# Two cross attentions in sequence: output products moved beside the last subtiles, folding of queries moved between stage 2's products

## The chip, the cores and the metric

The kernel runs on one core of one Trainium2 chip. The metric is the time of one execution in microseconds, measured on the device. All times below are microseconds unless marked ns. Engines are named as in the profile: PE (TensorE), DVE (VectorE), ACT (ScalarE), POOL (GpSimd), SP (SyncE, which here only issues DMAs).

## The reference

Two cross-attention layers follow each other on the same 4 x 64 context rows. All is float32; B = 4, 1024 query rows per batch, hidden size 1024.

```python
# layer 0: 32 query heads of 32, 8 key/value heads, biases, residual, layer norm
q = hidden @ Wq + bq; k = ctx @ Wk + bk; v = ctx @ Wv + bv
attn = softmax(q k^T / sqrt(32) + mask)          # 64 keys
x = (attn v) @ Wo + bo + hidden
x = (x - mean(x)) * rsqrt(var(x) + 1e-6) * gamma + beta
# layer 1: 16 heads of 64, context layer-normed, gated residual
a = layer_norm(ctx)
Q = x @ Wq1.T; K = a @ Wk1.T; V = a @ Wv1.T
attn = softmax(where(mask, Q K^T / 8, -inf))
y = x + tanh(gate) * (attn V) @ Wo1.T
```

## The kernel before

The 4096 rows are 32 subtiles of 128 (`t`), 16 pairs of two subtiles (`pair`), and 4 blocks of 8 subtiles, one batch each. The large products (1024 x 1024 by rows) are done in Winograd's form of Strassen's scheme: each 2 x 2 block product takes seven products instead of eight, with sums of blocks made ahead on DVE. `right_sums` makes the four sums of a weight, `left_out` the four of a left operand (128 x 512 each), and `products` lists the seven steps of one pair. A step is four 128-row matmuls over `HK`, each of which the profile records twice (so eight records), and then one DVE addition of the PSUM bank into the result rows `r` (L455). Three of the seven results are partial: the bank X takes four products on top of each other and is added to another quarter of the rows after each, V takes two, W one. A product that goes on in a bank must wait until DVE has read it.

The program runs in these parts.

- Setup: keys and values of both layers from the context.
- Stage 1: layer 0's queries for four blocks (`query_steps`, 28 steps a block). Beside the steps of blocks 1 to 3 run the attentions of subtiles 0 to 23.
- The last subtiles, 24 to 31: no query steps are left, so `other_work` gives them other steps.
- Stage 2: per pair the output projection of layer 0 (`project`, seven products with `w_o`), residual, bias and layer norm (`close_rows`), written to DRAM as `x1`.
- Stage 3: per pair layer 1's scores, softmax, and output. Layer 1's queries and keys are folded into one 1024 x 256 weight per batch (`ad`), its values and output weight into another (`bd`): `folded_queries` makes `ad`, `folded_values` makes `bd`.

`folded_queries(kT, wT, k)` handles one of eight chunks of 128 rows in four steps. A step has four matmuls on 64 partitions (two row halves side by side), 256 columns each, into two PSUM banks, two ACT copies out (L903), and, after every second step, a DMA of 1 MB to `ad` on POOL's queue (L909). `folded_values(vT, wch, c)` has two steps a chunk; each has two groups of two 64-partition matmuls with 512 columns (L924), four ACT copies (L929), and two DMAs on SP's queue.

`mix(t, count)` (L771) writes out one subtile of layer 0's attention and draws `count` steps of `other_work` at five places. A subtile's chain is: 16 score matmuls in two halves (`front`, L680, each followed by a DVE add with the mask, L684), the row maxima of both halves (`largest`, L691) and their subtraction (L694), exp on ACT, the row sums (`total`, L711), reciprocals and the division (`divide`, L715), the transposes of the previous subtile's probabilities on PE with copies by ACT (`flip`, L407 and L410), and the product with the values (L759) with two copies of ACT (L398) and a DMA. For some heads ACT does the subtraction itself, one head at a time, with the maximum as its bias, and sums up on the way (`some`, L698): the pair `alone` tells how many of the 16 heads of each half. In the last eight subtiles it is `(4, 0)`; the other heads go through DVE and one exp per half (`others`, L706).

`other_work` draws, after the query steps, 32 folding steps, eight of them before subtile 24 (`FOLD_AHEAD`), and then four products of pair 0 (`FIRST`). The loads of `w_o` (four blocks of 1 MB, four DMAs each, L147) are on SP's queue. After subtile 31 come pair 0's other three products, and then stage 2's loop from pair 1. In that loop `project` takes a list `fill` of small steps and runs a share of them after each product; the folding of values of chunk `pair - 1` (pairs 1 to 8) is part of that list.

PSUM has eight banks: `ps_big`, two tiles of two banks (scores, folding of values), and `ps_wx`, four tiles of one bank (products, folding of queries, transposes and values of the last subtiles). The weight pool has seven slots of 1 MB for tag `wa` (first `wq0`, then `wo0`) and seven for tag `wb`.

Instructions aren't issued in the order of the source: a scheduler orders them, engine by engine, by priorities and its own estimate of times, except where `keep_in_program_order` binds one.

Of the kernel before, what the change touches and what calls it, by code (L numbers as in the profile page):

```python
# [14 lines left out]
P = 128  # L15
# [4 lines left out]
B = 4  # L20
# [51 lines left out]
def tile_two_cross_attentions(  # L72
# [35 lines left out]
    ps_wx = ctx.enter_context(tc.tile_pool(name="ps_wx", bufs=4, space=bass.MemoryType.PSUM))  # L108
    ps_big = ctx.enter_context(tc.tile_pool(name="ps_big", bufs=2, space=bass.MemoryType.PSUM))

# [6 lines left out]
    def wx():  # L117
        return ps_wx.tile([P, 512], F32, tag="wx", name="wx")

# [21 lines left out]
    def block_of(w, i, j, tag, name, turned=False):  # L141
        t = new_block(tag, name)
        cols = slice(j * HW, (j + 1) * HW)
        if turned == "heads":
            rows = w.rearrange("(c g i e d) o -> c i e d g o", c=2, g=4, i=2, e=2)
            for a in range(NQ):
                nc.sync.dma_start(  # L147
                    out=t[a * Q : (a + 1) * Q], in_=rows[a // 2, a % 2, i][:, :, cols]
                )
# [285 lines left out]
    def products(a, w, r, bias=None, tail=None):  # L435
# [6 lines left out]
        def product(name, s, m, first, last):  # L442
            if first:
                banks[name] = wx()
# [33 lines left out]
        ]  # L478
        return [lambda o=o: step(*o) for o in order]

    def project(a, w, r, fill, bias=None, tail=None):

        share = -(-len(fill) // 7)
        for step in products(a, w, r, bias, tail):
            step()
            for _ in range(min(share, len(fill))):
                fill.pop(0)()
# [166 lines left out]
    def attend0(t):  # L654
# [13 lines left out]
        alone = BY_HEAD if by_turning(t) else (4, 0) if t >= NSUB - SUB else (0, 0)  # L668
# [218 lines left out]
    def folded_queries(kT, wT, k):  # L887
# [3 lines left out]
        def heads(cc):  # L891
            banks = [wx(), wx()]
# [47 lines left out]
    def load_o(pair, pool, tag="o2"):  # L940
        o = pool.tile([P, KC, 2 * P], F32, tag=tag, name=f"o2_{pair}")
        load = nc.sync.dma_start(out=o, in_=oTd[pair])
        if pair < 2:
            tc.keep_in_program_order(load)
        return o

    def load_outputs(pair):
        o = load_o(pair, o2pool) if pair > 1 else second if pair else load_o(0, early)
        r = []
        for u in range(2):  # L950
            t = pair * 2 + u
            ru = (rpool.tile([P, H], F32, tag="r", name=f"r_{t}") if pair
                  else early.tile([P, H], F32, tag="r", name=f"r_{t}", bufs=2))
            load = nc.sync.dma_start(out=ru, in_=x[sub_ap(t), :])
            if not pair:
                tc.keep_in_program_order(load)
            if pair:
                nc.gpsimd.tensor_tensor(ru, ru, bo_sb, ALU.add)  # L958
            r.append(ru)
        return o, r  # L960

    def other_work(rows):

        nonlocal fold, early, bo_sb, w_o, first, first_rows, second
# [12 lines left out]
        queries_cm.close()  # L977
        fold = open_pool(fold_cm, "fold", 1)

        early = open_pool(early_cm, "early", 1)  # L980
        kT = fold.tile([P, KC, B * S], F32, tag="kvT", name="kT")
        nc.sync.dma_start(out=kT, in_=kTd)
        wT = turned_chunk(0)
        w_o, w_o_loads = right_loads(wo0, "wa", "wo0", "heads")
        bo_sb = constant(bo0.partition_broadcast(P), [P, H], "bo", F32, fold)
        for k in range(KC):
            ahead = turned_chunk(k + 1) if k + 1 < KC else None
            for step in folded_queries(kT, wT, k):
                step()
                yield  # L990
            wT = ahead
            if k in (1, 2, 3, 4):
                w_o_loads[k - 1]()
            if k == 5:
                run(right_sums(w_o))
                o, first_rows = load_outputs(0)
                a = left_out(o, early, "0_0")
        second = load_o(1, wpool, "wb")

        def tail():  # L1000
            nonlocal ahead_a
            ahead_a = left_out(second, early, "0_1")


        first = products(a, w_o, first_rows, None, tail)
        for _ in range(FIRST):
            first.pop(0)()
            yield

    fold_cm, early_cm = ExitStack(), ExitStack()  # L1010
    fold = early = bo_sb = w_o = first = first_rows = second = ahead_a = ahead_r = None
    FIRST = 4
# [3 lines left out]
    AHEAD, FOLD_AHEAD = 4, 8  # L1016
# [11 lines left out]
    n = 4 * KC - FOLD_AHEAD + FIRST  # L1028
# [268 lines left out]
```

## Time and profile before

| what | us |
|---|---|
| median of three runs | 1914.9 (1913.46 to 1915.07) |
| the profiled execution | 1915.1 |
| its span, first to last instruction | 1913.3 |
| mean granted clock of PE | 0.995 of full |
| PE idle in the whole span | 44.4 |
| stage 1 with setup, to the first folding step | 0 to 588.9 |
| last subtiles, to subtile 31's last matmul of values | 588.9 to 716.4 |
| stage 2, to the last product of pair 15 | 716.4 to about 1185 |
| longest waits of PE: values for the transposed probabilities (DVE) | 6.2 in 5 |
| folding of queries for ACT's copies of transposes | 4.6 in 5 |
| folding of values for its own copies | 3.7 in 7 |

The profile is of one execution on the chip. A row of a group gives the source line, the engine, the operation, output and input tiles, shapes, the number of instructions, busy time and mean ns of one, the idle time ahead of them and who ended it. A row of the order in time gives start, duration, engine, line, operation and count; in brackets idle time before it and its releaser. PE's durations are modelled from pipelined records, so PE can look busy while it runs below its rate; the distance from one start to the next is the better measure.

### The profile page before, as it was taken

How to read it: one execution, taken by the hardware profiler on the slowest of the kernel's cores; microseconds unless marked ns; L12 is line 12 of the kernel's file. 1: busy time of each engine (PE TensorE's matmuls, PEld its weight loads, DVE VectorE, ACT ScalarE, POOL GpSimd, SP SyncE). 2: the span in 40 equal slices, each digit the busy share in tenths (PEclk: the TensorE clock that was granted, in tenths of full speed). 3: DMA queues.
4: the chain of work that ended last, by engine and by line, in shares of the span. 5: the costliest groups of instructions: out<-in, count | busy, mean ns of one | idle time of the engine just before them, and what ended most of it. 6: DMA issues, size and time to landing. Idle time of an engine off the chain costs nothing.

```text
span 1913.3 us, 17522 instructions
## 1 busy us (share of the span) xinstructions
PE 1868.9 (98%) x6096; PEld 880.0 (46%) x6096; DVE 1292.1 (68%) x1582; ACT 427.9 (22%) x1396; POOL 179.1 (9%) x212
## 2 busy tenths in 40 slices
PE   8999999999998899999999999999999999999999
PEld 7744444444455653343344444444444444444444
DVE  3425589789878985575568778557665766576653
ACT  1101575666536751212100001000000000000000
POOL 0016011111100103121113100000000000000000
PEclk9999999999999899999999999999999999999999
DMA  8996599899878966567473363466656565657421
GB/s 276 184 222 192 158 253 247 253 252 261 252 186 275 302 234 207 188 207 238 164 218 138 121 141 90 110 165 158 150 143 165 150 158 143 165 142 165 121 88 44
DMA packets 220745, 350.54 MB, mean 183 GB/s; under 512 B 26992, under 2 KB 146160, under 8 KB 215664
## 3 DMA queue, kind: packets, MB, share of 16 engines
q1 hardware_dynamic: 152896, 242.44, 45.8%
q0 software_dynamic: 15216, 60.83, 10.5%
q10 hardware_dynamic: 52544, 46.14, 8.8%
q8 instruction: 48, 0.79, 0.2%
q14 instruction: 41, 0.34, 0.1%
HBM read 207.53 MB, written 141.82 MB: 183 GB/s over the span
## 4 chain that ended last, share of the span: by engine, by line
PE 82%; DVE 8%; DMA 5%; issue 2%; ACT 2%; POOL 0%; SPq 0%; DVEq 0%; POOLq 0%; ACTq 0%
PE wx L446 59%; PE wx L576 14%; PE big L680 2%; DMA pq<-p 2%; PE big L924 1%; PE wx L379 1%; PE big L379 1%; DVE s L684 1%; PE big L759 1%; DMA p<-s 1%; DMA q<-qTd 1%; DVE s L715 1%; DVE mx L691 1%; DVE sm L711 1%; DMA o<-oTd 1%
## 5 line engine op out<-in xcount | busy, mean ns | idle before, releaser
L455 DVE TENSOR_TENSOR r<-wx,r 128x512 f32<-128x512 f32 x224 | 153.5, 686 | 230.1 <-PE wx L446 215.3
L698 ACT ACTIVATE s<-s,mx 128x64 f32<-128x64 f32 x488 | 162.8, 335 | 74.9 <-DVE mx L691 70.7
L502 ACT ACTIVATE s<-s 128x1024 f32<-128x1024 f32 x32 | 33.7, 1057 | 651.7 <-DVE s L501 651.7
L459 DVE TENSOR_TENSOR s<-wx,key_bias 128x512 f32<-128x512 f32 x64 | 44.1, 690 | 136.7 <-PE wx L446 136.7
L446 PE MATMUL wx<-wo_B,S 128*128 128x512 f32 x256 | 117.1, 600 | 1.5 <-DVE r L455 1.5
L576 PE MATMUL wx<-xT,wq_S 128*128 128x512 f32 x256 | 116.5, 598 | 0.8 <-ACT z L587 0.8
L446 PE MATMUL wx<-b_B,pT 128*128 128x512 f32 x256 | 115.8, 593 | 0.6 <-ACT pT L414 0.6
L446 PE MATMUL wx<-b_B,S_p 128*128 128x512 f32 x256 | 116.0, 596 | 0.0
L446 PE MATMUL wx<-a_B,xT 128*128 128x512 f32 x256 | 115.4, 592 | 0.0
L446 PE MATMUL wx<-a_B,S_x 128*128 128x512 f32 x256 | 115.3, 593 | 0.1
L576 PE MATMUL wx<-xB,wq_A 128*128 128x512 f32 x256 | 115.1, 597 | 0.0
L446 PE MATMUL wx<-wo_B,o 128*128 128x512 f32 x256 | 114.8, 596 | 0.0
L958 POOL TENSOR_TENSOR r<-r,bo 128x1024 f32<-128x1024 f32 x30 | 78.5, 2625 | 313.8 <-DMA r<-in_x_dram 159.4
L684 DVE TENSOR_TENSOR s<-big,m 128x1024 f32<-128x1024 f32 x64 | 77.4, 1215 | 28.4 <-PE big L680 26.8
L680 PEld LDWEIGHTS big<-kv,q 64*128 64x128 f32 x1024 | 71.1, 195 | 48.3 <-issue 39.9
L698 ACT ACTIVATION_READ_ACCUMULATOR s<-s,mx 128x1 f32 x488 | 91.4, 187 | 0.0
L680 PE MATMUL big<-kv,q 64*128 64x128 f32 x1024 | 82.6, 292 | 2.6 <-DMA q<-qTd 2.6
L419 DVE STREAM_TRANSPOSE pT<-pq 128x1024 f32<-128x1024 f32 x66 | 78.0, 1219 | 3.3 <-DMA pq<-p 3.3
L446 PEld LDWEIGHTS wx<-wo_B,S 128*128 128x128 f32 x256 | 47.1, 190 | 67.7 <-issue 51.2
L715 DVE TENSOR_TENSOR s<-s,sm 128x1024 f32<-128x1024 f32 x64 | 77.0, 1216 | 0.9
L446 PEld LDWEIGHTS wx<-wo_B,o 128*128 128x128 f32 x256 | 47.8, 190 | 63.5 <-issue 62.3
L446 PEld LDWEIGHTS wx<-a_B,S_x 128*128 128x128 f32 x256 | 48.5, 190 | 62.0 <-issue 58.4
(162 smaller groups left out, 2903.5 us busy)
## 6 DMA issues: line engine op xcount, KB each, us to landing
p<-s POOLq DMA_DIRECT2D x19, 1024.0 KB, 8.1
pq<-p POOLq DMA_DIRECT2D x76, 256.0 KB, 6.0
xq<-in_x_dram SPq DMA_DIRECT2D x64, 256.0 KB, 10.2
q<-qTd SPq DMA_DIRECT2D x32, 512.0 KB, 7.4
oTd<-oT ACTq DMA_DIRECT2D x32, 512.0 KB, 7.4
ad<-a POOLq DMA_DIRECT2D x16, 1024.0 KB, 8.9
o<-oTd SPq DMA_DIRECT2D x16, 1024.0 KB, 5.1
r<-in_x_dram SPq DMA_DIRECT2D x32, 512.0 KB, 5.3
```

The costliest lines, as they stand in the source:

```text
L379: nc.tensor.matmul(ps[:, 0:256], w[k // HK, c // HK][:, k % HK, sub_ap(c % HK)], ct[:, k, :], start=(k == 0), stop=(k == KC - 1),)
L419: return nc.vector.transpose(dst.rearrange("p k (u i) -> p k u i", i=Q), t[:, :, k0 * Q : k1 * Q].rearrange("p u (k j) -> p k u j", j=Q),)
L446: nc.tensor.matmul(banks[name], a[s][:, k, :], w[m][:, k, :], start=first and k == 0, stop=last and k == HK - 1, skip_group_check=True,)
L455: nc.vector.tensor_tensor(at, bank, at, ALU.add)
L459: nc.vector.tensor_tensor(at, bank.rearrange("p (h s) -> p h s", s=S), bias.unsqueeze(1).to_broadcast([P, 512 // S, S]), ALU.add,)
L502: nc.scalar.activation(s, s, AF.Exp)
L576: nc.tensor.matmul(bank, w_q[a][:, k, sub_ap(i)], rows[b][:, k, :], start=first and k == 0, stop=last and k == HK - 1, skip_group_check=True,)
L680: nc.tensor.matmul(ps[:, at : at + P], q[on, c * 4 + g, :], k0bd[on, b, c, :], start=True, stop=True,)
L684: nc.vector.tensor_tensor(quarters[:, :, c * 8 : (c + 1) * 8], ps.rearrange("p (k a l) -> p a k l", a=NQ, l=Q), mask.rearrange("p e (h l) ...
L698: nc.scalar.activation(heads[:, e, k], heads[:, e, k], AF.Exp, bias=mx[:, e, k : k + 1], accum_out=sm[:, e, k : k + 1],)
L715: nc.vector.tensor_tensor(heads[:, e], heads[:, e], wide(sm[:, e]), ALU.mult)
L958: nc.gpsimd.tensor_tensor(ru, ru, bo_sb, ALU.add)
```

## The change

- Between stage 1 and the last subtiles PSUM's four `wx` banks are shared out anew (`share_banks`): three for `wx` and one, `sum_bank`, for the products; from stage 2 on, four for `wx` again.
- The last subtiles take 12 of 32 folding steps (`FOLDED` = 3 chunks, four steps of them before subtile 24 instead of eight), and then products of pairs 0 and 1: seven and four (`BESIDE` = 2, `LEFT` = 3 left over). Their order puts X's four products in a row, then V's two, then W, so that one bank is open at a time (`one_bank`). The last three products of pair 1 stand around subtile 31's transposes and values.
- Stage 2's loop starts at pair 2. Folding of queries for chunks 3 to 7 goes there, in pairs 3 to 7: one step after each of four products, in the `big` banks. Folding of values goes to pairs 3 to 10, one step after each of two products (`beside`), and no longer through `fill`.
- `alone` is `(8, 4)` for the last subtiles: 12 of 32 heads are taken one at a time by ACT.
- The loads of `w_o` go to POOL's queue. The residual rows of pairs 0 and 1 are one DMA of 1 MB each into a `wb` slot, as are the left operands of pairs 0 to 2. `vT` has a tile of its own; the pools of stage 3 that took the place of `early` open at pair 11 instead of 3, and the first load of `ad` moves from pair 10 to 11.

```diff
+    def share_banks(name, sums):
+        nonlocal ps_wx, ps_sum
+        ps_cm.close()
+        ps_wx = ps_cm.enter_context(
+            tc.tile_pool(name=f"ps_wx{name}", bufs=4 - sums, space=bass.MemoryType.PSUM, reuse_waits="tile")
+        )
+        ps_sum = sums and ps_cm.enter_context(
+            tc.tile_pool(name=f"ps_sum{name}", bufs=sums, space=bass.MemoryType.PSUM, reuse_waits="tile")
+        )
+    def sum_bank():
+        return ps_sum.tile([P, 512], F32, tag="sum", name="sum") if ps_sum else wx()
...
-                nc.sync.dma_start(
+                nc.gpsimd.dma_start(
                     out=t[a * Q : (a + 1) * Q], in_=rows[a // 2, a % 2, i][:, :, cols]
...
-                banks[name] = wx()
+                banks[name] = sum_bank()
...
+        if one_bank:
+            order = [order[i] for i in (0, 1, 3, 4, 2, 5, 6)]
...
-        for step in products(a, w, r, bias, tail):
+        for i, step in enumerate(products(a, w, r, bias, tail)):
             step()
+            if i in beside:
+                beside[i]()
...
-        alone = BY_HEAD if by_turning(t) else (4, 0) if t >= NSUB - SUB else (0, 0)
+        alone = BY_HEAD if by_turning(t) else (8, 4) if t >= NSUB - SUB else (0, 0)
...
-            banks = [wx(), wx()]
+            banks = two() if pairs else [wx(), wx()]
...
+        share_banks("1", 1)
...
-        for k in range(KC):
+        for k in range(FOLDED):
-            for step in folded_queries(kT, wT, k):
+            for n, step in enumerate(folded_queries(kT, wT, k)):
                 step()
+                if k > 0 and n % 2 and sums:
+                    sums.pop(0)()
                 yield
...
+        for step in products(a, w_o, first[0][1], None, tail, True):
+            step()
             yield
+        for step in products(ahead_a[0], w_o, first[1][1], None, tail1, True):
+            steps.append(step)
+        while len(steps) > LEFT:
+            steps.pop(0)()
+            yield
+        rest.extend(steps)
...
-    AHEAD, FOLD_AHEAD = 4, 8
+    AHEAD, FOLD_AHEAD = 4, 4
...
+    counts = [4, 4] + [(i + 1) * (7 * BESIDE - LEFT) // 6 - i * (7 * BESIDE - LEFT) // 6 for i in range(6)]
     for i in range(SUB):
-        mix(last + i, (i + 1) * n // SUB - i * n // SUB)
+        mix(last + i, counts[i])
...
+    fill = close_with_bias(0, first[0][1]) + close_with_bias(1, first[1][1])
+    FROM = BESIDE + 1
-    for pair in range(1, NPAIR):
+    for pair in range(BESIDE, NPAIR):
...
+        beside = {}
+        k = pair - FROM + FOLDED
+        if pair >= FROM and k < KC:
+            ahead_w = turned_chunk(k + 1) if k + 1 < KC else None
+            beside.update(zip((0, 2, 3, 5), folded_queries(kT, wT, k, True)))
+            wT = ahead_w
+        k = pair - FROM
+        if 0 <= k < KC:
+            ahead_w = chunk(wo1, k + 1, "wo1") if k + 1 < KC else None
+            beside.update(zip((1, 4), folded_values(vT, wch, k)))
+            wch = ahead_w
...
-        project(a, w_o, r, fill, tail=tail)
+        project(a, w_o, r, fill, tail=tail, beside=beside)
```

## The prediction

> **What bounds the kernel now.** I read the engines' shares first, then the stretches around the change, then the order in time on VectorE and TensorE, then the waits.
>
> ```profile
> PE 1868.9 (98%) x6096; PEld 880.0 (46%) x6096; DVE 1292.1 (68%) x1582; ACT 427.9 (22%) x1396; POOL 179.1 (9%) x212
> ...
> 617.60:629.50 11.90, 10.87 (x100) 8.35 (x99) 11.34 (x12) 10.63 (x26) 1.51 (x2) 1.00 0.94 314
> 669.60:681.50 11.90, 10.78 (x99) 8.26 (x98) 11.31 (x13) 10.58 (x26) 1.50 (x2) 1.00 1.00 313
> 775.20:804.60 29.40, 28.87 (x73) 11.68 (x72) 16.38 (x25) 5.25 (x10) 5.66 (x2) 1.00 0.66 211
> ```
>
> The columns of a stretch are its length and then busy time of PE, weight loads, DVE, ACT, POOL. PE looks full everywhere, but in the last eight subtiles (590 to 716 us) that is stretched work: in 11.9 us DVE is busy 11.3. In stage 2 (the third stretch, one pair) DVE has 13 us to spare and PE none. So PE work that moves from stage 2 into the last subtiles is free as long as DVE, or the loop through ACT, isn't lengthened.
>
> One subtile on DVE, from row maximum to row maximum:
>
> ```profile
> 669.63 2.35 DVE L691 TENSOR_REDUCE mx<-s 128x16 f32<-128x1024 f32 x2
> 671.90 2.08 DVE L694 TENSOR_TENSOR s<-s,mx 128x768 f32<-128x768 f32 x2
> 674.53 2.17 DVE L711 TENSOR_REDUCE sm<-s 128x12 f32<-128x768 f32 x2 [0.55 <-ACT s L706]
> 676.62 0.37 DVE L712 RECIPROCAL sm<-sm 128x16 f32<-128x16 f32 x2
> 676.90 2.35 DVE L715 TENSOR_TENSOR s<-s,sm 128x1024 f32<-128x1024 f32 x2
> 679.17 2.35 DVE L684 TENSOR_TENSOR s<-big,m 128x1024 f32<-128x1024 f32 x2
> 681.55 2.35 DVE L691 TENSOR_REDUCE mx<-s 128x16 f32<-128x1024 f32 x2
> ```
>
> It takes 11.92: 11.1 of work and 0.85 of waits, 0.55 of them for ACT. The first maxima of subtiles 24 to 31 start at 602.3, 617.6, 629.5, 641.5, 658.1, 669.6, 681.6, 694.1: seven periods, 91.7 together, with a late load of q in the first and the sums of pair 0's left operand in the fourth. ACT has, in the same region:
>
> ```profile
> L903 ACT ACTIVATE a<-wx 128x512 f32<-128x512 f32 x64 | 33.7, 610 | 18.3 <-PE wx L897 13.9 <-DMA ad<-a 4.3
> L410 ACT COPY pT<-wx 128x512 f32<-128x512 f32 x32 | 16.9, 584 | 6.7 <-PE wx L407 6.7
> L698 ACT ACTIVATE s<-s,mx 128x64 f32<-128x64 f32 x32 | 10.8, 340 | 12.2 <-DVE mx L691 12.0
> L706 ACT ACTIVATE s<-s 128x768 f32<-128x768 f32 x8 | 6.8, 853 | 0.0
> ```
>
> And stage 2's joints, PE in order of time, with the wait that its folding of values has:
>
> ```profile
> 734.95 1.12 PE L924 MATMUL big<-wo,vT 64*128 64x512 f32 x2
> 736.01 3.70 PE L446 MATMUL wx<-wo_B,S 128*128 128x512 f32 x8
> 739.64 1.98 PE L924 MATMUL big<-wo,vT 64*128 64x512 f32 x6
> 741.55 3.70 PE L446 MATMUL wx<-wo_N,o 128*128 128x512 f32 x8
> ...
> 777.71 2.28 PE L924 MATMUL big<-wo,vT 64*128 64x512 f32 x8 [0.51 <-ACT b L929]
> ...
> PE big L924 <- ACT b L929: 3.7, 7, 0.6
> ```
>
> A product is eight matmul records. Seven of them take 24.67 in a pair without joints, 3.525 each; between two groups of 64-row matmuls one takes 3.63 (736.01 to 739.64), so a joint costs 0.1. Eight records of values take 1.92 standing alone, 2.97 when cut into 2 and 6 (1.06 + 1.91), and two groups in a row 4.74 with their wait, against 3.84.
>
> **The change, part by part.**
>
> *The last subtiles, in DVE's time.* Four heads fewer in both halves: a subtraction or sum takes 1.218 on 16 heads and 0.948 on 12, so 0.27 per four heads, four times a subtile: work falls from 11.1 to 10.0. Added: eleven sums of products instead of three before subtile 31's division (8 x 0.61 spacing), left operands of three pairs instead of one (8 more operations of 0.61, since the changed order brings pair 2's in too), and two bias adds (1.2 each) and three small statistics steps that the order pulls in: 4.9 + 4.9 + 3.9. Eight subtiles save 8.6 and take 13.7.
>
> *The loop through ACT.* ACT takes twelve single heads instead of four, at a spacing of 0.335 (timeline of ACT, 642.70 to 644.05 for four). From the end of a subtile's first maximum: four exps 1.34, three copies of transposes 1.42 (three follow in 1.42 at 684.15), the exp on 12 heads 0.78, the fourth copy 0.5, which now comes after it, because only three banks are left for four transposes; half of the values' matmuls 0.5, the rest of the next scores 0.3, hand-overs 0.25: the next first score add can start at 5.1, where DVE has been idle for some 0.5. From there one add 1.14, division 1.14, the sum on eight heads 0.6 (ACT is ready at 7.3), reciprocal 0.15, product sum 0.6, division, add and maximum 3.4: 12.15 a period. Walking the changed order through with those prices, the periods are 12.4, 15.9, 12.4, 14.2, 13.8, 13.9, 12.6, together 95.2. The second has ACT still folding (four steps, 4 x 1.0), pair 0's left operand and the first product's sum; the fourth five left-operand steps; the fifth and sixth the bias adds and statistics. DVE's own work and waits without the loop give about the same, 7 x 12.0 + 11.5 = 95.5. So +3.5.
>
> *The start* gains little: four folding steps fewer stand ahead of subtile 24 (PE is through at 593.8, not 597.7), but q was issued at 592.1 and landed no sooner than 5.6 later, and DVE had the weight sums until 597.6. I take -0.8, bounds 0 and -1.1 (DVE's idle time there).
>
> *The tail*, end of subtile 31's first maximum to its last values matmul: 21.1 before (695.3 to 716.4), full of five products. Now 16.9: division at 709, transposes 1.9, three quarters of a product 2.6, values 1.0. So -4.2; the stretch ends 1.5 earlier, and holds 13 products instead of six and 13 folding steps instead of 32.
>
> The sqrt of pair 0 gets between the exps of subtiles 30 and 31: two table loads of 1.28 (the row has one, after the last subtile), 3.3 with the sqrt and a DMA issue, in a gap of 4.2 before the next exp: hidden. The Trainium skill, "ScalarE: Activation LUTs", What ACT_TABLE_LOAD costs, adds a drain of about 1.4 to each: as an estimate two switches are then 5.3, 6.0 with the rest, the exps start 1.8 late, and the sum below would be -3.3; no row here shows the drain.
>
> *Stage 2.* Seven products leave: -24.7. Nineteen folding steps come: alone they took 0.96 to 1.00 (600.85 to 601.84), with a joint half the values' 1.92 would be 0.96, cut in two as the values are 1.49. I take 1.03, since all but one stand whole: +19.5, up to +28. Some 33 more joints at 0.106: +3.5, bounds 0 and 5. Values: chunks 1 to 4 lose their wait (4.74 to 3.84), chunks 5 to 7 are cut twice each in the changed order (4.74 to 5.94), the first loses a little: -0.9. The 0.97 that PE waited for POOL's bias add (L958) goes, as one folding piece more stands before it: -1.0, bound 0. Sum -3.6. DVE and ACT in this stage have 13 and 24 us of 29 free per pair; the 10 writes of `ad` (1 MB each) fall where the DMA share is 0.4 to 0.66. Each chunk is loaded a pair ahead. All value tiles share one slot; a write to `bd` has 6 to 8 us of slack before its slot is needed.
>
> *Queues.* The sixteen loads of wo0 go from SP to POOL. Four POOL loads issue in 2.18; POOL has nothing between 525 and 593, so 8.7 fit. One stands ahead of subtile 18's reads of `pq`; SP issued it at 523.4, the reads came at 525.4, so nothing, or 2 if the slot is late. SP loses a wait of 5.6 (four loads from 534.7) with `qTd` writes behind it: 0 to -2. Zero for both. On SP five loads of 1 MB now stand ahead of subtile 28's q; they have two periods, 24 us, for 13 us of DMA at 390 GB/s.
>
> **Sum.** -1.5 - 3.6 = -5.1: span 1908.2, and with the 1.8 around it (1915.1 measured, span 1913.3) 1910.0. The median of the runs shown is 0.2 below that execution, which is less than I can resolve.
>
> **Rivals.**
>
> *The loop decides and the kernel gets slower.* For: TensorE, DVE, ACT and PE's one sum bank now wait on each other in a ring, with 12 exps, three banks and two products per subtile; before, transposes' copies already held folding up 4.6 us in 5 waits, 0.92 each. If every subtile has one such wait and the spacings are the full durations (periods 13.7, 17.1, 13.2, 14.6, 13.8, 14.1, 12.9, which end the stretch 2.9 late), it is +2.9 + 7.4 - 3.6 = +6.7: 1921.8. Against: most pieces have been seen to overlap. It is slower from a mean period of 14.3 on (13.6 in my walk).
>
> *VectorE runs without waits.* Fillers fall into its gaps, seven waits of 0.85 go: -6: 1904. Against: front adds still need PE.
>
> *Stage 2 gives it back.* Folding steps run one row half after the other, or wait for a copy; with half of the 0.46 extra each, +4.4 and the total is 1914.4, no change. For: three chunks of values are cut that way. Against: the folding steps stand whole, and copies (2 x 0.6) have a product's 3.5.
>
> *It doesn't do what it says*: the order shows twelve products ahead of the last subtile's transposes, so this I leave out.
>
> **How the numbers follow.** Forecast 0.43, its own range 1905 to 1914; slower loop 0.28; free VectorE 0.16; stage 2 gives back 0.13. No change is within 0.2%, 3.8 us, about what runs of this kernel can tell. Faster: 0.33 of the forecast's 0.43, the 0.16 and 0.01: 0.50. Slower: 0.28, 0.02 of the forecast and 0.01 of the third: 0.31. Same: 0.19. The range, 1901 to 1921, takes in the free VectorE with a late SP gain, and nearly the whole loop.
>
> **What would show it.** Maxima (L712 after) of subtiles 24 to 31 at a mean period near 13.6; the last values matmul near 715; 32.5 us a pair in pairs 4 to 7 of stage 2 with no wait at the values; waits of PE for POOL gone. Wrong if the mean period is over 14.3 or under 12.8, if folding steps in stage 2 take over 1.3, or if PE there waits for ACT or a DMA.

## The result and the profile after

The changed kernel is slower: 1923.87 us median of four runs (1923.08 to 1927.25) against 1914.18 of the kernel before (1913.14 to 1915.07); the ratio is 1.0053, with a 95% interval of 1.0038 to 1.0068. The forecast was 1910.0, so the sign was wrong. The profiled execution of the changed kernel is its longest, 1927.25 with a span of 1925.5; against the span of before, 1913.3, the trace has 12.2 to explain, 2.5 more than the medians differ. The medians further down leave out one run of 4908.11 (products cut to a quarter) and one of 7491.70 (copies first with whole values).

The engines' shares on the page come first:

```profile
PE 1884.2 (98%) x6096; PEld 874.3 (45%) x6096; DVE 1275.8 (66%) x1584; ACT 449.8 (23%) x1526; POOL 180.2 (9%) x226
```

TensorE has the same 6096 records as before and is busy 15.3 longer: the same work was done more slowly or behind waits that a busy time doesn't show. Cut by events, the trace gives this:

| stretch | before | after | change | forecast |
|---|---|---|---|---|
| to the first maximum of subtile 24 | 602.3 | 604.7 | +2.3 | -0.8 |
| from there to the first maximum of subtile 31 | 91.7 | 104.4 | +12.7 | +3.5 |
| from there to subtile 31's last values | 22.3 | 18.4 | -3.9 | -4.2 |
| stage 2, to the first product of stage 3 | 413.6 | 414.5 | +0.9 | -3.6 |

The second row by periods, in stretches of the changed kernel. The columns are length, busy time and count of PE, weight loads, DVE, ACT and POOL, then granted clock, DMA share and GB/s:

```profile
604.66:618.79 14.13, 13.20 (x97) 8.49 (x95) 10.77 (x12) 12.55 (x39) 1.51 (x2) 0.88 0.73 260
618.79:639.24 20.45, 17.17 (x96) 10.33 (x96) 13.77 (x17) 11.08 (x39) 1.50 (x2) 0.83 1.03 370
639.24:651.69 12.45, 11.53 (x74) 5.96 (x72) 12.42 (x18) 8.04 (x32) 0.00 (x0) 1.00 0.80 265
651.69:666.60 14.91, 14.71 (x83) 7.56 (x82) 14.27 (x21) 8.21 (x32) 0.00 (x0) 1.00 0.53 158
666.60:681.29 14.69, 14.17 (x82) 7.29 (x81) 12.90 (x17) 8.30 (x32) 0.00 (x0) 1.00 0.27 76
681.29:695.73 14.44, 13.60 (x81) 6.93 (x80) 13.74 (x19) 8.21 (x32) 0.00 (x0) 1.00 0.32 86
695.73:709.06 13.33, 12.60 (x78) 6.53 (x77) 11.92 (x18) 10.98 (x35) 0.00 (x0) 1.00 0.14 40
```

VectorE is busy 89.8 of these 104.4; before it was 82.6 of 91.7. So 7.2 of the 12.7 are VectorE's added work, and 5.5 are added waits of VectorE. The first two periods hold 7.4 of the growth and all of the added waits: VectorE waits 10.0 in them, against 4.5 before. In the last five, VectorE's work grew by 5.3 (59.9 to 65.2), as much as their length (64.5 to 69.8), and its waits stayed at 4.6. TensorE is idle for only 3.2 of these five, and two engines that both look full are where a busy time tells least. The order in time on TensorE in one of them:

```profile
666.94 1.93 PE L423 MATMUL wx<-ident,s 128*128 128x128 f32 x16
668.80 0.93 PE L701 MATMUL big<-kv,q 64*128 64x128 f32 x10
670.02 1.55 PE L780 MATMUL wx<-pT,kv 64*32 64x512 f32 x12 [0.28 <-ACT pT L426]
671.81 1.05 PE L780 MATMUL wx<-pT,kv 64*32 64x512 f32 x4 [0.23 <-ACT pT L426]
672.79 0.71 PE L701 MATMUL big<-kv,q 64*128 64x128 f32 x6
673.42 3.70 PE L462 MATMUL sum<-wo_N,o 128*128 128x512 f32 x8
677.05 1.16 PE L701 MATMUL big<-kv,q 64*128 64x128 f32 x16
678.15 3.70 PE L462 MATMUL sum<-wo_B,o 128*128 128x512 f32 x8
```

The values (L780) reach from 670.02 to 672.79, where the next work starts, though their 16 records took 1.09 where nothing held them (before, at 673.90). ACT in the same period, without its single exps, shows what they wait for:

```profile
667.58 0.58 ACT L426 COPY pT<-wx 128x512 f32<-128x512 f32 x1 [6.44 <-PE wx L423]
...
669.40 1.05 ACT L426 COPY pT<-wx 128x512 f32<-128x512 f32 x2
670.44 0.84 ACT L727 ACTIVATE s<-s 128x768 f32<-128x768 f32 x1
671.19 0.57 ACT L426 COPY pT<-wx 128x512 f32<-128x512 f32 x1
```

ACT had been idle for 6.44, did one copy, then four single exps (668.06 to 669.40), two copies, the exp on 12 heads and only then the fourth copy. In this trace TensorE runs scores and products only behind the last values, in the order in which they were queued. Stage 2 has other waits of TensorE than before; they are listed by who waited for whom, in total, times and longest:

```profile
PE wx L462 <- DVE r L471: 3.6, 5, 1.3
PE wx L462 <- DVE o L447: 1.5, 1, 1.5
```

The 3.7 for the copies of the folded values are gone, as forecast; 5.1 for VectorE stand there now, against 2.5 before.

### The profile page after: what moved, and what is told of

It reads as the page before. It is cut to its first block, busy times and chain, and to the rows that moved or that the text cites. A ratio compares the mean times of both kernels' runs of the same rounds, so it can differ in the third digit from the quotient of the medians.

```text
span 1925.5 us, 17681 instructions
## 1 busy us (share of the span) xinstructions
PE 1884.2 (98%) x6096; PEld 874.3 (45%) x6096; DVE 1275.8 (66%) x1584; ACT 449.8 (23%) x1526; POOL 180.2 (9%) x226
## 3 DMA queue, kind: packets, MB, share of 16 engines
q0 software_dynamic: 16496, 65.02, 11.3%
## 4 chain that ended last, share of the span: by engine, by line
PE 83%; DVE 9%; DMA 3%; ACT 2%; issue 2%; POOL 0%; DVEq 0%; SPq 0%; POOLq 0%; ACTq 0%
PE wx L462 55%; PE wx L597 15%; PE big L701 2%; PE big L945 2%; PE sum L462 2%; PE wx L395 1%; PE big L395 1%; PE big L780 1%; DVE s L705 1%; PE big L918 1%; DMA pq<-p 1%; DVE s L736 1%; DVE mx L712 1%; ACT s L719 1%; PE wx L780 1%
## 5 line engine op out<-in xcount | busy, mean ns | idle before, releaser
L471 DVE TENSOR_TENSOR r<-wx,r 128x512 f32<-128x512 f32 x210 | 143.7, 685 | 240.8 <-PE wx L462 240.4
L719 ACT ACTIVATE s<-s,mx 128x64 f32<-128x64 f32 x552 | 184.3, 337 | 84.1 <-DVE mx L712 79.8
L462 PE MATMUL wx<-wo_B,S 128*128 128x512 f32 x224 | 102.9, 602 | 3.4 <-DVE r L471 3.4
L719 ACT ACTIVATION_READ_ACCUMULATOR s<-s,mx 128x1 f32 x552 | 104.2, 189 | 0.0
L979 POOL TENSOR_TENSOR r<-r,bo 128x1024 f32<-128x1024 f32 x28 | 71.0, 2543 | 342.6 <-DMA r<-in_x_dram 321.4
L462 PE MATMUL wx<-wo_B,o 128*128 128x512 f32 x224 | 99.2, 595 | 0.0
L701 PEld LDWEIGHTS big<-kv,q 64*128 64x128 f32 x1024 | 67.0, 191 | 50.4 <-issue 42.0
L462 PEld LDWEIGHTS wx<-a_B,xT 128*128 128x128 f32 x256 | 48.6, 190 | 61.2 <-issue 60.5
L462 PEld LDWEIGHTS wx<-b_B,S_p 128*128 128x128 f32 x256 | 47.6, 190 | 63.3 <-issue 51.6
```

The costliest lines, as they stand in the source:

```text
L462: nc.tensor.matmul(banks[name], a[s][:, k, :], w[m][:, k, :], start=first and k == 0, stop=last and k == HK - 1, skip_group_check=True,)
L471: nc.vector.tensor_tensor(at, bank, at, ALU.add)
L701: nc.tensor.matmul(ps[:, at : at + P], q[on, c * 4 + g, :], k0bd[on, b, c, :], start=True, stop=True,)
L719: nc.scalar.activation(heads[:, e, k], heads[:, e, k], AF.Exp, bias=mx[:, e, k : k + 1], accum_out=sm[:, e, k : k + 1],)
```

## The experiments

Ratios are to the kernel before, run beside each on the same chip. "Five periods" are those from subtile 26 to 31. An edit also changes which of VectorE's steps the scheduler puts there, so their length is read beside VectorE's busy time:

| kernel | five periods | VectorE busy | VectorE waits |
|---|---|---|---|
| before | 64.5 | 59.9 | 4.6 |
| changed | 69.8 | 65.2 | 4.6 |
| small work kept out | 68.3 | 62.2 | 6.0 |
| products cut to a quarter | 61.4 | 56.8 | 4.6 |
| four heads on ACT | 71.1 | 68.1 | 3.1 |
| seven products | 56.4 | 56.2 | 0.1 |
| copies first | 64.3 | 64.0 | 0.3 |
| copies first, whole values | 68.0 | 64.3 | 3.7 |

### Four parts taken back one at a time

**Small work kept out of the last subtiles** (bias adds, statistics of pair 0):

```diff
-            lambda u=u: nc.vector.tensor_tensor(r[u], r[u], bo_sb, ALU.add) for u in range(2)
+            lambda u=u: tc.keep_in_program_order(nc.vector.tensor_tensor(r[u], r[u], bo_sb, ALU.add)) for u in range(2)
```

> The changed kernel, with the two bias adds of each of pairs 0 and 1 kept behind the work that stands ahead of them in the source: about 4 us of VectorE's work (two adds of 1.22, statistics of 0.68 twice, small steps) leave subtiles 28 to 31 and come back in stage 2's first pairs. Theory A (TensorE's own queue sets the subtiles with two products: transposes 1.93, scores 2.3, two products 7.25, values 2.64 of which 1.55 are waits for ACT's copies, 14.1 in all): the periods from subtile 28 on stay within 0.5 each, and the total within 2 us of the changed kernel. Theory B (VectorE's added work sets them: 7.2 of the 12.7 by which the seven periods grew): the periods from 28 to 31 shrink by some 3.8 together, and the total falls by 2 to 4.

1925.57, ratio 1.0058 (1.0043 to 1.0074). The periods from 28 on fell by 1.6 together, for 3.0 of VectorE's work that left the five, and stage 2 grew from 414.5 to 419.6: the same steps stand there ahead of the products' sums. TensorE's waits in it:

```profile
PE wx L462 <- DVE r L471: 7.1, 5, 2.8
```

The fall lies between the two theories (two of the periods moved by more than A's 0.5, and B had 3.8). So VectorE's work alone doesn't set these subtiles, and it isn't free in stage 2's first pairs either.

**Products cut to a quarter:**

```diff
-            for k in range(HK):
+            for k in range(1 if ps_sum else HK):
...
```

> The changed kernel, but each product that is written into the one sum bank (all of pairs 0 and 1) does one of its four matmuls: three quarters of those products are left out, so the output isn't the reference's. VectorE's and ACT's work stays. Theory A (TensorE's queue sets the subtiles with products): TensorE has 8.7 us of work in them instead of 14.1, and the periods fall from 14.4 to VectorE's pace, about 12.2, so 6 to 10 less from subtile 25 to 31, and 8 less in the products after the last maximum: total 14 to 20 below the changed kernel. Theory B (VectorE's work and its ring with ACT): the periods of subtiles 28 to 31 stay above 13.8, and only the products after the last maximum shrink: total 8 to 10 below.

This kernel leaves out three quarters of those products. It took 1917.10, ratio 1.0010 (0.9998 to 1.0022): 6.8 below the changed kernel, and the total missed both ranges. The five periods, changed kernel first:

```profile
639.24:709.06 69.82, 66.61 (x390) 34.27 (x388) 65.25 (x86) 43.74 (x163) 0.00 (x0) 1.00 0.41 122
632.56:693.96 61.40, 48.16 (x343) 28.76 (x341) 56.78 (x72) 40.99 (x159) 0.00 (x0) 0.88 0.47 151
```

They fell by 8.4, which is theory A's number, but VectorE's work in them fell by as much (65.25 to 56.78), and its waits stayed: the scheduler put bias adds, statistics, one left operand and one division behind the last maximum, where the stretch to the last values didn't shrink (18.7 against 18.4). So this run doesn't separate the theories. With 37 us less for TensorE to do, its granted clock fell to 0.83 to 0.93 in these periods.

**Four heads on ACT instead of twelve:**

```diff
-        alone = BY_HEAD if by_turning(t) else (8, 4) if t >= NSUB - SUB else (0, 0)
+        alone = BY_HEAD if by_turning(t) else (4, 0) if t >= NSUB - SUB else (0, 0)
```

> The changed kernel with four heads of one half on ACT, as before, instead of eight and four. VectorE gets 1.1 us more a subtile, ACT eight exps (2.7 us) fewer. Theory A with ACT ahead of TensorE's values: the copies of transposes come up to 1.3 sooner, values take 1.1 to 1.5 instead of 2.64, and a subtile with two products gets 0.5 to 1.5 shorter: total 0 to 8 below the changed kernel. Theory B: each period gets 1.1 longer, total 4 to 8 above the changed kernel.

1923.34, ratio 1.0045 (1.0030 to 1.0060); the seven periods 104.2, as in the changed kernel. VectorE has 4.1 more work in them and waits 4.3 less: what it gains by the change of heads goes into added waits. Neither theory's larger number came.

**No bank apart:** `share_banks("1", 0)` instead of `("1", 1)`.

> The changed kernel, without the bank set apart for the products: all four single banks are shared by products, transposes, values and folding in the last subtiles, as before. Theory C (three banks are too few: the fourth transpose copy stands behind the exp on 12 heads, and half of the values wait for it): values in one go, about 1 a subtile less, total 4 to 8 below the changed kernel. Against it: a product holds a bank of the four at nearly all times, and its bank comes back only when VectorE has added it; then the total stays within 2 of the changed kernel.

1923.01, ratio 1.0042 (1.0026 to 1.0059): within 1 of the changed kernel. Three banks are not the cause.

### Loads, start, number of products

**The first loads one subtile earlier:** `load_o(0)` and `load_rows(0)` ahead of the third folding chunk.

> The changed kernel, with the loads of pair 0's left operand and rows issued one subtile earlier, ahead of q of subtile 27 instead of behind its masks. In the changed kernel the period from subtile 25 to 26 takes 20.45: VectorE waits 1.99 and TensorE 2.27 for that load, which was issued at 620.70, and the next product takes 6.44 at a granted clock of 0.5 to 0.6. Theory A (the late load is a loss of its own): this period falls to 14 to 16, total 4 to 6 below the changed kernel. Rival (the wait moves: the five loads of 1 MB then delay q, or the sums of the left operand alone fill the period): the period stays above 18, or a later one grows, total within 2.

1924.76, ratio 1.0055 (1.0034 to 1.0076). The period from 25 to 26 fell from 20.45 to 17.13, with a wait of TensorE of 3.24 for ACT's copies in it, and the one ahead of it rose from 14.13 to 17.63: the sums of pair 0's operand, and VectorE's wait for its load (2.32), now stand there. The wait moved, as the rival had it.

**Eight folding steps ahead of subtile 24:** `FOLD_AHEAD = 8`, counts `[2, 2]`.

> The changed kernel, with eight folding steps ahead of subtile 24 as before the change, and two instead of four in each of subtiles 24 and 25. Theory: four steps are too few to cover the way of the last queries through DRAM, and TensorE waits 1.95 for q of subtile 24; with eight it has work meanwhile, and the four steps leave subtiles 24 and 25. First maximum of 24 at most 1 later, periods 24 to 26 shorter by 3 to 4 in all: total 2 to 4 below the changed kernel. Rival: TensorE's work is only put elsewhere and the ring with VectorE sets those two periods anyway: total within 1.5.

1928.59, ratio 1.0073 (1.0058 to 1.0088). The two periods after 24 got 3.2 shorter as expected, but its first maximum came at 611.4 instead of 604.7, behind a wait of TensorE of 4.18 for the weights of folding. Both expectations were wrong.

**Seven products instead of eleven beside the subtiles:** `LEFT = 7`.

> The changed kernel, with all seven products of pair 1 after the last subtile's steps (four more than now), and seven of pair 0 in six subtiles instead of eleven products. Theory A (TensorE's work adds to these subtiles, and a product costs there nearly what it costs anywhere): periods from 26 to 31 fall from some 14 to 11.5 to 12.5, about 10 to 13 in all, and the four products take 14.1 behind them: total within 3 of the changed kernel. Theory B (the ring of VectorE and ACT sets the periods, products fit in beside it): periods fall by at most 4 (four sums and four operand steps), and the total is 8 to 12 above the changed kernel.

1928.99, ratio 1.0074 (1.0057 to 1.0090). The five periods fell from 69.8 to 56.4:

```profile
634.43:690.80 56.37, 51.26 (x363) 28.65 (x360) 56.23 (x72) 41.03 (x160) 0.00 (x0) 1.00 0.47 145
```

Of these 13.4, 9.0 are VectorE's work that left with the four products (their sums, bias adds, statistics) or fell behind the last maximum, and 4.4 are waits: VectorE then had no gap. The periods are near what theory A has, but VectorE's work went with TensorE's, so this run can't tell them apart. The total rose by 5.1, outside both ranges: behind the subtiles pair 1's products share the one sum bank in a row, and each waits for VectorE to empty it:

```profile
PE sum L462 <- DVE r L471: 6.6, 4, 3.1
```

**The loads of `wo0` on SP again:**

```diff
-                nc.gpsimd.dma_start(
+                nc.sync.dma_start(
                     out=t[a * Q : (a + 1) * Q], in_=rows[a // 2, a % 2, i][:, :, cols]
```

> The changed kernel with the sixteen loads of wo0 on SP's queue again. The first folding step started at 588.7 to 591.3 in nine profiles of the changed kernel and its variants (mean 590.2), at 588.9 and 587.5 in two of the kernel before. Theory (the loads on POOL's queue delay stage 1's end): the first folding step starts at 587.5 to 589, total 1.5 to 3 below the changed kernel. Rival (the order of stage 1 changed for other reasons, or it is spread): 589.5 to 591.5, total within 1.5.

1927.49, ratio 1.0065 (1.0040 to 1.0089), first folding step at 590.1: nothing was won back, so the queue isn't shown to cost anything.

**Pair 0's operand loaded before the folding, in the kernel before:**

> The kernel before, with pair 0's left operand and rows loaded before the first folding chunk instead of in the sixth. Theory: its sums on VectorE (2.7) then fall where VectorE waits for the first scores of subtile 24, and the period that held them (16.64 from 27 to 28, with 1.40 of wait for the load) falls to 12: last subtiles 3 to 4.5 shorter, total 2 to 5 below the kernel before. Rival: what these periods lose comes back because the folding or the queries are late for it (DMA share is 1.0 there): total within 2.

1916.91, ratio 1.0018 (1.0007 to 1.0028). The period of 16.64 became 11.92, and all from 25 on took 11.9 to 12.5; but the load came in front of the weights of folding, TensorE waited 6.61 for those, and subtile 24's first maximum was 5.5 later.

### Folded values one step at a time

**The change's stage 2 placement alone, in the kernel before:**

```diff
-            fill += folded_values(vT, wch, pair - 1)
+            beside.update(zip((1, 4), folded_values(vT, wch, pair - 1)))
```

> The kernel before, with one edit of the change alone: the two steps of folded values of a pair stand after its second and fifth product, and not in the list of small steps. Theory: the second group of values no longer waits for ACT's copy of the first (7 waits of 0.51 to 0.56), eight chunks lose 4.74 - 3.84 = 0.9 each unless they are cut: total 3 to 6 below the kernel before. Rival: chunks are cut in two by products, as chunks 5 to 7 were in the changed kernel (5.94 instead of 4.74): total within 2 of the kernel before.

1923.9, ratio 1.0050 (1.0035 to 1.0065): slower by as much as the whole change, against my expectation and beyond the rival's. Of TensorE in order of time, in one pair:

```profile
783.03 1.12 PE L926 MATMUL big<-wo,vT 64*128 64x512 f32 x2
784.08 3.70 PE L446 MATMUL wx<-wo_T,S 128*128 128x512 f32 x8
787.71 1.98 PE L926 MATMUL big<-wo,vT 64*128 64x512 f32 x6
```

The scheduler put a product between a group's first matmul and the other three. A group is two pairs on the two row halves. Two records alone take 1.05, the other six 1.91, the eight together 1.92: a half that has lost its partner costs as much as both. A pair of subtiles takes 30.75 instead of 29.38, eight times.

**The same with the matmuls kept in the order of the source**, in both kernels:

```diff
-                    nc.tensor.matmul(
+                    tc.keep_in_program_order(nc.tensor.matmul(
                         banks[e], vT[q, c, sub_ap(bp)], wch[q, n * 512 : (n + 1) * 512],
```

> The kernel before with the folded values beside the second and fifth product, as in the run that took 30.75 a pair, and with their matmuls kept in the order of the source, so that the two row halves of a group follow each other directly. Theory (two 64-row matmuls on different row halves run in the time of one, 1.05, and a product between them costs the second its partner: groups of 2 and 6 records take 1.05 and 1.91, one of 8 takes 1.92): a pair takes 24.67 + 2 x 1.92 + 0.2 to 0.4 = 28.7 to 28.9 instead of 29.38 before and 30.75 cut: 4 to 6 below the kernel before. Rival (separate groups cost something else, such as the switch between 64-row and 128-row work): a pair stays above 30, total 6 to 10 above the kernel before.

> The changed kernel with the matmuls of the folded values kept in the order of the source. Only chunks 0 and 5 to 7 were cut in it (pairs 8 to 10: 30.75 to 30.85). Theory of the cut halves: these three pairs fall to 28.7 to 28.9, total 5 to 7 below the changed kernel, stage 2 at 408 to 410 instead of 414.5. Rival: unchanged within 2.

The kernel before with it, in one pair:

```profile
868.34 3.70 PE L446 MATMUL wx<-wo_T,S 128*128 128x512 f32 x8
871.97 1.99 PE L926 MATMUL big<-wo,vT 64*128 64x512 f32 x8
873.88 2.84 PE L446 MATMUL wx<-wo_T,o 128*128 128x512 f32 x6
```

A pair now takes 28.72 and the kernel 1912.3, ratio 0.9988 (0.9977 to 1.0000), less of a gain than the 4 to 6 expected; TensorE waits 2.2 longer for VectorE's sums, which takes a part back. The changed kernel with it takes 1919.27, ratio 1.0027 (1.0018 to 1.0036), and stage 2 410.1: 4.6 of its loss are the cut groups, just under the 5 to 7 expected.

### Copies ahead of the exps

**ACT's order turned** (the flip's three lines go away further down; the products come out in other places too):

```diff
         front(1)
+        plain = t and not by_turning(t - 1)
+        if plain and t - 2 not in turned:
+            flip(t - 1)
         largest(0)
...
-                nc.scalar.copy(
+                tc.keep_in_program_order(nc.scalar.copy(
...
-                nc.scalar.activation(
+                tc.keep_in_program_order(nc.scalar.activation(
```

> The changed kernel with ACT's order in the last subtiles turned: the copies of the previous subtile's transposes stand ahead of the single exps, and the products come out of it placed so: transposes, product, values, scores, product, scores. Theory A (TensorE's own work in a subtile with two products is 1.93 + 3.63 + 1.09 + 1.09 + 3.63 + 1.09 = 12.5, and the rest of 14.4 is its wait for copies that stand behind 4 and then 1 exps on ACT): values in one go of 1.1, periods from 26 on of 12.5 to 13.3, total 5 to 9 below the changed kernel. Rival (VectorE's added work and the ring with the exps, now started 2 later, set the period): periods stay at 13.8 or more, total within 3.

1922.76, ratio 1.0039 (1.0026 to 1.0052). TensorE in one subtile with two products, and the five periods in stretches (DVE is the third busy time):

```profile
671.93 1.96 PE L423 MATMUL wx<-ident,s 128*128 128x128 f32 x16 [0.68 <-DVE s L736]
673.73 3.60 PE L462 MATMUL sum<-wo_B,o 128*128 128x512 f32 x8
677.26 1.09 PE L780 MATMUL wx<-pT,kv 64*32 64x512 f32 x16
678.28 1.16 PE L701 MATMUL big<-kv,q 64*128 64x128 f32 x16
679.37 3.70 PE L462 MATMUL sum<-wo_B,o 128*128 128x512 f32 x8
683.00 1.16 PE L701 MATMUL big<-kv,q 64*128 64x128 f32 x16
```

```profile
635.87:648.22 12.35, 11.32 (x78) 6.13 (x77) 12.35 (x17) 7.64 (x32) 0.00 (x0) 1.00 1.03 320
648.22:661.13 12.91, 11.59 (x82) 6.85 (x81) 12.91 (x19) 9.64 (x36) 0.00 (x0) 1.00 0.41 122
661.13:674.82 13.69, 13.01 (x83) 7.06 (x82) 13.62 (x19) 9.18 (x34) 0.00 (x0) 1.00 0.33 92
674.82:688.40 13.58, 11.56 (x79) 6.30 (x78) 13.58 (x19) 8.06 (x32) 0.00 (x0) 1.00 0.31 85
688.40:700.15 11.75, 11.69 (x79) 6.37 (x78) 11.57 (x17) 9.51 (x35) 0.00 (x0) 1.00 0.16 45
```

The values stand in one go of 1.09 behind a product that hides the copies; the five periods fall from 69.8 to 64.3, and VectorE, with nearly the same steps as in the changed kernel, is busy 64.0 of them: now it alone sets them. This is the run that shows that the waits for copies were real. Right behind them lies VectorE's added work, which the rival named; each of the two theories was right about one of two limits that lie 5 us apart. The total falls by 1.1 only. Stage 2 began with a wait of 2.61 for VectorE and took 418.6.

**With whole values as well**, in the changed kernel and in the one before:

> The same, and with the folded values whole as well, as in the run that measured 1.0027. If both losses are what they seem and add up, 4 to 5 below the kernel with the copies first alone; with theory A on that one this is 1910 to 1914, at or just below the kernel before. Rival: stage 2 then waits more for VectorE, and the two together give less than 3 more than the copies alone.

> The kernel before with the folded values whole beside two products, and with the copies of transposes ahead of the single exps. VectorE sets its last subtiles (11.1 of work in 11.92), so at most the 0.55 that it waits for ACT in each can go: theory: total within 2 of the kernel with whole values alone (0.9988), since nothing that binds changes. Rival: copies first delay the exps, VectorE waits longer for them, periods of 12.5 to 13: 4 to 8 slower.

The changed kernel with both takes 1913.95, ratio 1.0000 (0.9989 to 1.0010): the whole loss of 9.7 is back, though the two edits alone gave 1.1 and 4.6, so they don't simply add up. In its profile the five periods take 68.0:

```profile
636.02:704.06 68.04, 60.76 (x395) 33.22 (x394) 64.30 (x85) 43.86 (x164) 0.00 (x0) 0.97 0.46 144
```

TensorE waits 3.59 in them for q of subtile 28 and VectorE 3.3 for a product. Against the profile of the changed kernel, 10.5 longer, the seven periods give back 4.3 (2.9 of them from 25 to 26), stage 2 3.7, the stretch behind the last maximum 1.7, and the start 0.7. The kernel before with both takes 1914.14, ratio 0.9999 (0.9990 to 1.0008), no better than with whole values alone.

**Loads spread as well:** `load_o(1)` and `load_rows(1)` ahead of the third product, `load_o(2)` behind pair 0's last, `vT` kept behind it; in the second kernel pair 0's loads also one chunk earlier.

> The changed kernel with copies first and whole values (1914.6 in the run before), and its 1 MB loads spread: pair 1's operand and rows behind the queries of subtile 28, pair 2's operand behind the last masks, vT behind that, instead of all ahead of the queries of 28. There TensorE waited 3.59 for q of 28 and VectorE then 3.26 for a product. Theory (those loads, which I had priced at no wait, cost a wait as soon as the loop is faster): the wait for q goes, the periods from 25 to 28 (17.54, 12.35, 16.66) fall by 4 to 6, total 3 to 6 below, 1908 to 1912. Rival: the loads meet the stage 2 start instead (rows, gamma, beta, the first wo chunk), and what is gained comes back there: within 2.

> The same with pair 0's operand and rows one subtile earlier. Theory: the first product's wait for its operand in the period from 25 to 26 goes too, another 1 to 3 less. Rival: q of 27 then comes late behind these 2 MB, as the period from 24 to 25 grew when only this was done (17.63 instead of 14.1): within 2 of the other.

1916.33, ratio 1.0009 (0.9999 to 1.0019), and 1916.93, ratio 1.0010 (1.0000 to 1.0021). The wait for q of 28 went, but the period from 25 to 26 took 23.6 and 23.9: TensorE's granted clock was 0.50 for 13.65 of it (here in the first).

```profile
621.82:635.47 13.65, 13.65 (x49) 7.03 (x42) 7.03 (x10) 5.20 (x17) 0.75 (x1) 0.50 0.79 291
```

What makes this period long (16.0 to 23.9 in all variants) stays open; the late load is not it alone. The two variants whose clock was full in it took 16.0 (four heads on ACT) and 17.5 (copies first with whole values). In the second of the two kernels here the runs go from 1911.88 at a mean clock of 0.997 to 1922.15, the profiled one, at 0.992. That points at the clock; but with the load one subtile earlier the period took 17.1 at a mean of 0.80, and no run holds the clock fixed.

**The faster version once more:**

> The kernel before with whole values beside two products once more, in more rounds, since its interval (0.9977 to 1.0000) touched no change. Theory: each of eight pairs takes 28.72 instead of 29.38, 5.3 in all, and TensorE waits 2.2 longer for VectorE's additions: 2 to 4 below, ratio 0.998 to 0.999. Rival: the difference was the spread of the runs: 0.9993 to 1.0007.

1911.45 against 1913.83, ratio 0.9986 (0.9977 to 0.9994): the kernel before, with the folded values whole beside two products, is the one version that beats both.

## Why the prediction was wrong, point by point

*VectorE's work* was sized nearly right: 7.2 more in the seven periods; the forecast had 5.1 in eight subtiles (13.7 less 8.6). *Its waits were not*: the walked periods, 95.2, leave 5.4 beside the 89.8 of work, and 14.6 came. This is the step that failed, and the rows show it in two places.

The first two periods were put at 28.3 and took 34.6, which is 6.3 of the 9.2. The second was put at 15.9 and took 20.45:

```profile
632.04 0.69 DVE L445 TENSOR_TENSOR S<-o 128x512 f32<-128x512 f32 x1 [1.99 <-DMA o<-oTd]
638.64 0.69 DVE L471 TENSOR_TENSOR r<-sum,r 128x512 f32<-128x512 f32 x1 [2.96 <-PE sum L462]
```

VectorE waited 1.99 and TensorE 2.27 for the operand `o`, for which the walk had no wait (the prediction asked only whether the loads delay q of subtile 28); the product behind it took 6.44 instead of 3.6 at a granted clock of 0.50, and VectorE waited 2.96 for it. Loading it one subtile earlier only moved the wait, so why these two periods are long stays open.

The five later periods were put at 66.9 and took 69.8, the other 2.9. The walk let half of the values (0.5) follow the fourth copy. It had the copies' place right, but not that TensorE's queue stands still with them: values reach over 2.64 to 2.77 in four of the five, instead of 1.09. With the copies first these five took 64.3.

*The premise* that TensorE's work is free there as long as VectorE or the loop through ACT isn't lengthened was too easy: 12.5 of TensorE's own work in a subtile with two products (1.93 + 7.26 + 1.09 + 2.2) is longer than the 11.92 of before. With the copies first, where little else holds it up, TensorE is idle for 5.1 of the 64.3 and VectorE for 0.3, so there VectorE's work sets the pace after all.

*The start* (-0.8) came out at +2.3. All of it lies ahead of the first folding step (591.3, against 588.9): from there to the first maximum both kernels take 13.4 to 13.5. First folding steps lie between 587.5 and 591.3 in all profiles, and between 588.1 and 591.3 in variants with the same stage 1, so it may be spread. The queue of `wo0`, priced at zero, isn't shown to be the cause, and more folding ahead made the first maximum later.

*The tail* was right: -4.2 forecast, -3.9 measured. The table loads for pair 0's square root ended at 708.0, 2.31 before ACT's next exp: hidden, as forecast. Load, root and load start at 705.21, 706.50 and 706.72: no drain of 1.4, as in the prediction's estimate, stands behind the first load of 1.28.

*Stage 2* was 4.5 off. The products (-24.7) and the steps' price were right: a pair with four folding steps and two groups of values takes 33.31 (my "32.5" had left out six joints that the sum held). The waits for copies went. What failed is "DVE has 13 us free per pair": in the first pairs two closings stand ahead of the sums, and TensorE waits 5.1 for VectorE in the stage instead of 2.5; some 1.5 of the 4.5 stays open. The cut groups in pairs 8 to 10, which I read from the order and priced at 5.94 a chunk, measured 6.1 (30.75 less 24.67). So they explain loss against the kernel before, and next to nothing of the miss. But I took them as a detail: kept whole they give 4.6 back.

*The rivals.* The slower loop, 1921.8 from a mean period of 14.3 on, was the one that came: 14.9. Its mechanism, copies of transposes that hold up TensorE, was named and measured. Its sum for the last subtiles, 2.9 + 7.4 = 10.3, lies near the 11.1 that came, and what it missed of the total is stage 2. That it fits is in part luck: it spread one wait of 0.92 over every subtile, but the five later periods have no more waits of VectorE than before, and the excess lies in the first two. In the third rival the row halves of cut groups were named for the folding steps; they came in the values, at the price that the forecast had.

## What to carry to other kernels

Where two engines both look full, find out what the one's queue stands behind: move the producer's work (here copies ahead of exps), and the wait or the next limit shows itself. When an experiment shortens a stretch, look at what else left it: here two edits to TensorE's work took 8.5 and 9.0 of VectorE's along. Before work is moved into a stage, add up every engine's own work there in time from start to start; here VectorE was already busy 11.3 of 11.9 in a subtile. And when a scheduler may interleave, keep groups that run together on the array in one piece, and look at the order for single halves.

## What the runs showed of the hardware

TensorE's granted clock falls to 0.50 in blocks. In the changed kernel, around the late operand:

```profile
632.10:635.30 3.20, 3.14 (x4) 1.51 (x5) 3.20 (x5) 0.00 (x0) 0.00 (x0) 0.50 1.02 416
```

```profile
632.16 6.44 PE L462 MATMUL sum<-wo_B,o 128*128 128x512 f32 x8 [2.27 <-DMA o<-oTd]
```

The product takes 6.44 instead of 3.6. Summed over stretches of 1 us from 560 to 780, the clock that was not granted comes to 1.7, 3.4, 5.1, 6.8, 8.5, 11.9, 13.7 or 15.4 in the profiles of all kernels here: multiples of 1.7, blocks of 3.4 at half rate. The kernel before has 8.5, the changed one 6.8, so the sum isn't the difference between them; where the blocks fall can be, since before a period at a mean clock of 0.70 (658 to 670) took 11.54 and in the changed kernel a product on the way took 6.44. The kernel with products cut to a quarter has 15.4, a likely reason why less work gave back so little: its fastest run, 1911.12, has the highest mean clock, 0.993, and those at 0.987 to 0.989 take 1917.10 to 1921.34. The Trainium skill, "TensorE: Matmul & The Clock Gate", Part 1: The HAM clock gate, says that the clock goes to half after an idle window of about 3.4 us and back after a busy one; the size of the blocks agrees, but waits here are often shorter. The longest waits of TensorE that begin in the 6.8 us ahead of the changed kernel's three stretches at 0.50 are 1.95, 0.93 and 2.27, and 0.96 ahead of the 13.65 at 0.50 in the first kernel with loads spread.
